# Sinkhorn chains regrouped: one GpSimd chain for six row tiles, joined in stages, and VectorE for the last four

## The chip, the core and the metric

The kernel runs on one core of one Trainium2 chip. A core has five engines with an instruction stream each: TensorE (PE, matmuls; PEld is its weight load), VectorE (DVE), ScalarE (ACT), GpSimd (POOL) and SyncE (SP, which issues the DMAs here). Every engine works off its own stream in order; an instruction that needs another engine's result waits for it, and everything behind it on its engine waits too.

The metric is the device time of one execution in microseconds (us), the median of several runs. The kernel before takes 1380.76 us (median of 3 runs, 1379.34 to 1381.67).

## The reference

The function is two transformer layers with adaptive layer norm, on x of two rows (batch entries) of 512 tokens by 512 channels. Layer 0 is a gated chunked linear attention and a sign-weight feed-forward; layer 1 is a softmax attention with 32 heads of width 16, and at its end a "hyper-connection" feed-forward with a Sinkhorn normalisation. Only that last part is touched here:

```python
def sinkhorn_log(logits, num_iters=50, tau=0.1):
    Z = logits / tau
    u0 = jnp.zeros(Z.shape[:-1], Z.dtype); v0 = jnp.zeros_like(u0)
    def step(carry, _):
        u, v = carry
        u = -jax.nn.logsumexp(Z + v[..., None, :], axis=-1)
        v = -jax.nn.logsumexp(Z + u[..., :, None], axis=-2)
        return ((u, v), None)
    (u, v), _ = jax.lax.scan(step, (u0, v0), None, length=num_iters)
    return jnp.exp(Z + u[..., :, None] + v[..., None, :])
...
x_norm = x * jax.lax.rsqrt(jnp.mean(x * x, axis=-1, keepdims=True) + RMS_EPS)
H_res  = sinkhorn_log((x_norm @ W_res.T).reshape(B, T, 4, 4) + H_res_base)
H_pre  = softmax(x_norm @ W_pre.T + H_pre_base);  H_post = softmax(x_norm @ W_post.T + H_post_base)
H_res  = (1 - g) * I + g * H_res                       # g = sigmoid(gate)
y      = einsum('btnc,btn->btc', x_streams, H_pre) @ W_branch
out    = einsum('btij,btjc->btic', H_res, x_streams) + einsum('btc,btn->btnc', y, H_post)
```

Every token has a 4 by 4 matrix, and 50 iterations turn it into a nearly doubly stochastic one. The result mixes the token's four streams of 128 channels.

## The kernel before

**Tiles and halves.** The 1024 tokens are eight tiles of 128 tokens (tokens on the partitions, 512 channels along the free axis), four for each batch row. The last part works on halves of a row, two tiles each. They are called A0 and A1 here (row 0, first and second half) and B0 and B1 (row 1).

**The order of the work.** Layer 1's attention runs over 16 steps in `order`, for row 0 and then row 1, in each for the first half of the queries and then the second. `piece()` issues one eighth of a step: score matmuls (L861) whose row maxima VectorE takes (L865), transposed score matmuls (L899) whose exponentials ScalarE takes (L904, shown as L78 with the tile `pt`), and the matmuls with the values (L919). After the last piece of a quarter, `weighed()` (L1357) puts the generator of that half's last part into the list `side` (L1379): `streams0` for A0 and A1, `streams1a` for B0, `streams1b` for B1. After every piece, `aside(2)` takes up to two steps (up to a `yield`) of each generator in the list, under `tc.high_priority(400)`. Instructions are so written in this order, and the framework's scheduler then lays out each engine's stream from its own model of times, by priority.

**One half's last part.** `opening` (L1001) makes the logits: transposes and matmuls on TensorE, statistics on VectorE, two small powers on GpSimd (L134, L135). With `last` the layer norm of the half is on VectorE (L1038, L1039), otherwise partly on GpSimd. `first_iteration` (L1115) does the first of the 50 iterations with logarithms and leaves a positive 4 by 4 matrix K per token. `branch` (L1053) is the branch with `W_branch`. `iterations` (L1141) does the other 49 in scaled form: fa = 1 / row sums of K fb, fb = 1 / column sums of K fa. `result` (L1178) makes the mixing matrix, and `mixed_on_tensor` (L1206) mixes one tile: for each of the 16 matrix entries ScalarE writes a diagonal 128 by 128 matrix (L1196) and TensorE multiplies it with a stream (L1217); with four more for the branch where that has not been added before (`branch_on_tensor`, L1198). `put` (L1188) multiplies with the gate on VectorE (L1191), adds the residual on GpSimd or VectorE (L1192) and stores the tile by a DMA on SP's queue.

**One iteration.** With `last` it is all on VectorE: multiply (L1164), sum (L1154), reciprocal (L1166), multiply (L1168), sum (L1154), reciprocal (L1170). Otherwise the multiplications are on GpSimd, and each sum is two additions there (L1157 for pairs, L1158 for the pairs' sums); only the two reciprocals are on VectorE. Such a GpSimd iteration is 6 GpSimd and 2 VectorE instructions and 4 hand-overs between the engines. Two tiles make operands of 32 elements per partition for K, 16 for the pairs, 8 for a factor. After the iterations in `renew` (16 and 32) K is made anew from the logits (`kernel_of`, L1146) with two Ln and an Exp on ScalarE.

**Who does which chain.** A0 and A1 are two separate GpSimd chains of 49 iterations on two tiles, each with a room of its own in memory (`chain_room`, L1093). B0 does iterations 1 to 16 alone on VectorE (`streams1a`). Then B0 and B1 share a room and 33 iterations on four tiles on VectorE (B0's 17 to 49 and B1's 1 to 33, L1289), and B1 does its last 16 alone (L1293). Behind B1's result one tile is mixed on TensorE and the other on VectorE (L1237) from a branch part that ScalarE has left in `foutb` (L1230).

Of the kernel before, what the change touches and what calls it, by code (L numbers as in the profile page):

```python
# [9 lines left out]
FP = mybir.dt.float32  # L10
# [6 lines left out]
UPS = 400, 400, 400, 400  # L17
RATES = None, None, None, None
HEAD = 16
UP = 400  # L20
RAW = 4
POP = 1
# [14 lines left out]
P = 128  # L37
B, L, HID = 2, 512, 512
NC = L // P
# [13 lines left out]
def tile_adaln(ctx: ExitStack, tc: tile.TileContext, a: dict, out: bass.AP):  # L53
# [117 lines left out]
    def temp(shape, dt, name, bufs=2):  # L171
        return wk.tile(shape, dt, name=name, bufs=bufs)
# [917 lines left out]
    over = lambda t: t.unsqueeze(3).to_broadcast(list(t.shape) + [NS])  # L1090
    along = lambda t: t.unsqueeze(2).to_broadcast([t.shape[0], t.shape[1], NS, NS])

    def chain_room(n, last):  # L1093

        room = temp([P, 512], FP, "sinkhorn", 4)
        used = [0]

        def carve(shape):
            m = int(np.prod(shape[1:]))
            t = room[:, used[0]:used[0] + m]  # L1100
            used[0] += m
            if len(shape) == 4:
                return t.rearrange("p (c i j) -> p c i j", i=NS, j=shape[3])
            return t.rearrange("p (c i) -> p c i", i=NS)

        R = {k: carve([P, n, NS, NS]) for k in ("z", "t", "y", "K")}
        R.update({k: carve([P, n, NS]) for k in ("mx", "s", "u", "v", "fa", "fb", "fl")})
        if not last:
            R["pairs"] = carve([P, n, NS, 2])
        return R  # L1110

    def part(R, lo, hi):
        return {k: t[:, lo:hi] for k, t in R.items()}

    def first_iteration(S, R):  # L1115
        z, t, y, K, mx, s_, u, v, fl = (R[k] for k in ("z", "t", "y", "K", "mx", "s", "u", "v", "fl"))
# [61 lines left out]
    def result(S, R):  # L1178

        hr, n = R["y"], S["n"]  # L1180
        nc.vector.tensor_tensor(hr, R["K"], over(R["fa"]), ALU.mult)
        nc.vector.tensor_tensor(hr, hr, along(R["fb"]), ALU.mult)
        hrf = hr.rearrange("p c i j -> p c (i j)")
        for c in range(n):
            nc.vector.scalar_tensor_tensor(hrf[:, c, :], hrf[:, c, :], gt[:, 0:1], diag, ALU.mult, ALU.add)
        S["hr"] = hr
# [55 lines left out]
        put(S, c, ff, ff, nc.gpsimd)  # L1242
        yield

    RENEW = 16, 32

    def streams0(c0):

        S = {"b": 0, "c0": c0, "n": 2}
        yield from opening(S, False)  # L1250
        R = chain_room(2, False)
        yield from first_iteration(S, R)
        yield from S["branch"]
        yield from iterations(R, range(1, NITER), RENEW, False)
        result(S, R)
        for c in range(2):
            yield from mixed_on_tensor(S, c, nc.gpsimd)

    joint = {}

    def streams1a():

        S = joint["a"] = {"b": 1, "c0": 0, "n": 2}
        yield from opening(S, True)
        R = joint["R"] = chain_room(4, True)
        yield from first_iteration(S, part(R, 0, 2))
        yield from S["branch"]
        yield from iterations(part(R, 0, 2), range(1, HEAD + 1), (HEAD,), True)

    def streams1b(ahead):  # L1270

        S = {"b": 1, "c0": 2, "n": 2}
        yield from opening(S, True)
        yield from ahead
        A, R = joint["a"], joint["R"]
        yield from first_iteration(S, part(R, 2, 4))

        def branches():
            yield from S["branch"]
            branch_on_tensor(S, 1)  # L1280
            yield
            branch_on_scalar(S, 0)
            yield
            for c in range(2):
                branch_on_tensor(A, c)
                yield

        side.append((1, branches(), UP))
        yield from iterations(R, range(1, NITER - HEAD), RENEW, True)  # L1289
        result(A, part(R, 0, 2))  # L1290
        side.append((None, mixed_on_tensor(A, 0, nc.gpsimd), UP))
        side.append((None, mixed_on_tensor(A, 1, nc.gpsimd), UP))
        yield from iterations(part(R, 2, 4), range(NITER - HEAD, NITER), RENEW, True)  # L1293
        result(S, part(R, 2, 4))
        last = [mixed_on_tensor(S, 1, nc.vector), mixed_on_vector(S, 0)]
        while last:
            for e in list(last):
                if next(e, "end") == "end":
                    last.remove(e)
            yield  # L1300
# [56 lines left out]
    def weighed():  # L1357
        w = wt[0]
        wt[0] += 1
        if w < n_pieces:  # L1360
            if w == n_pieces // 2:
                values1(1)
            weigh(order[w // 8], w % 8)
        o = w - OUT
        if 0 <= o < n_pieces and o % 4 == 3:
            outputs(o // 4)
        o -= 5
        if o >= 0 and o % 4 == 0 and o < n_pieces:
            j = o // 4
            finish(j)  # L1370
            if j % 16 == 5:
                with behind():
                    row_tiles(j // 16, (SB, CB, GB))
                    weights24(j // 16)
            if j % 8 == 7:
                k = j // 8
                if k == 2:
                    joint["ahead"] = streams1a()
                side.append((RATES[k], (streams0(2 * k) if k < 2 else joint["ahead"] if k == 2 else streams1b(joint["ahead"])), UPS[k]))  # L1379

    virtual = []
    load_stationary("wk0", 0, 0)
# [167 lines left out]
```

## Time and profile before

The profiled execution took 1379.86 us; its span, from the first to the last instruction, is 1378.0 us, so 1.9 us lie around it. All times below count from the span's start.

| event (profiled execution) | start, us |
|---|---|
| first GpSimd iteration of A0 (L1157) | 1093.16 |
| first GpSimd iteration of A1 (L1157) | 1172.59 |
| K of B0 there (L1136) | 1230.73 |
| iteration 33 of A0 (L1157) | 1243.90 |
| last matmuls with the attention's values (L919) | 1254.09 |
| K of B1 there (L1136) | 1267.94 |
| first joint sum of B0 and B1 (L1154, 128x64) | 1271.34 |
| A0's result (L1181) | 1291.19 |
| B0's result (L1181) | 1335.89 |
| A1's result (L1181) | 1339.96 |
| B1's result (L1181) | 1363.74 |
| last arithmetic instruction (L1192) | 1374.45 |
| end of the span | 1378.0 |

A timeline row reads: start, duration, engine, line, operation, out<-in, shapes of the output and the first input, count of merged instructions, and in brackets the idle time before it on its engine and what ended that. A row of the windows reads: the window, its length, and for each engine the busy microseconds and the number of instructions in it, then TensorE's granted clock and the DMA share.

### The profile page before, as it was taken

What the parts mean: (1) busy time and instruction counts of PE and PEld (TensorE: products, weight loads), DVE (VectorE), ACT (ScalarE), POOL (GpSimd) and SP (SyncE); (2) the same over time, 40 slices, a digit from 0 to 9 for tenths busy, and PEclk for the clock granted to TensorE, in tenths of its full rate; (3) what the DMA queues carried; (4) which work ended last, traced back from release to release, by engine and by line L of the source; (5) the groups of instructions that cost most, each with busy time, mean ns of one, the idle gap of its engine ahead of it and who ended that gap; (6) DMA issues with size and microseconds to landing.
All of it is one profiled execution on the core that took longest, in us unless ns stands there. A gap on an engine that the chain in (4) does not pass through costs nothing.

```text
span 1378.0 us, 22951 instructions
## 1 busy us (share of the span) xinstructions
PE 1249.1 (91%) x7224; PEld 1001.1 (73%) x7224; DVE 1109.9 (81%) x2732; ACT 847.2 (61%) x2384; POOL 783.8 (57%) x1218
## 2 busy tenths in 40 slices
PE   5989999999999999999989999699999999996308
PEld 2767888788788787888877887577777777764308
DVE  7999677787686778877989876577869889898887
ACT  5457576476366466766666665465758678775407
POOL 4465274365266367667788947634335755668651
PEclk9999999999999999999999999899999999997758
DMA  7122241231133143333443326613203321200001
GB/s 246 37 66 51 80 133 40 69 108 54 47 92 93 54 146 92 100 85 100 123 129 94 102 68 206 205 46 110 84 25 120 98 88 49 65 14 2 9 8 47
DMA packets 96369, 116.61 MB, mean 85 GB/s; under 512 B 12076, under 2 KB 51756, under 8 KB 96248
## 3 DMA queue, kind: packets, MB, share of 16 engines
q1 hardware_dynamic: 96248, 115.15, 27.8%
q8 instruction: 57, 0.93, 0.3%
q14 instruction: 64, 0.52, 0.1%
HBM read 101.59 MB, written 10.64 MB: 81 GB/s over the span
## 4 chain that ended last, share of the span: by engine, by line
PE 61%; DVE 16%; POOL 11%; DMA 4%; issue 4%; ACT 3%; SPq 1%; POOLq 0%; ACTq 0%; DVEq 0%
PE pps L251 12%; PE ops L251 10%; PE gps L251 9%; PE op L919 4%; PE s L899 4%; PE s L861 4%; PE yps L567 3%; PE mix L1217 3%; PE sps L251 2%; PE yps L569 2%; DVE m L865 2%; PE cps L251 2%; PE mps L290 1%; PE ztp L585 1%; POOL q L466 1%
## 5 line engine op out<-in xcount | busy, mean ns | idle before, releaser
L865 DVE TENSOR_REDUCE m<-s 128x1 f32<-128x512 f32 x256 | 165.4, 672 | 23.7 <-PE s L861 23.2
L78 ACT ACTIVATE pt<-s 128x512 f32<-128x512 f32 x256 | 138.0, 599 | 14.9 <-PE s L899 13.6
L466 POOL TENSOR_TENSOR q<-xcos,rot 128x512 f32<-128x512 f32 x64 | 92.5, 1445 | 60.4 <-DVE xcos L464 58.8
L78 ACT ACTIVATE sg<-sg 128x512 f32<-128x512 f32 x128 | 80.9, 633 | 61.2 <-DVE sg L497 59.3
L861 PE MATMUL s<-ks,qs 96*128 96x512 f32 x256 | 104.2, 438 | 10.0 <-DVE m L865 5.2
L251 PE MATMUL pps<-hh,wq_h 128*128 128x512 f32 x256 | 103.7, 405 | 3.4 <-ACT vT L785 3.2
L78 ACT ACTIVATE dec<-dec,room 128x128 f32<-128x128 f32 x256 | 82.9, 398 | 35.2 <-POOL dec L514 35.1
L251 PE MATMUL ops<-wo_h,zh 128*128 128x512 f32 x256 | 102.1, 399 | 0.7 <-DVE zl L590 0.7
L251 PE MATMUL ops<-wo_h,zl 128*128 128x512 f32 x256 | 101.7, 397 | 0.9 <-DVE zl L590 0.9
L251 PE MATMUL pps<-hl,wq_h 128*128 128x512 f32 x256 | 101.7, 397 | 0.0
L251 PE MATMUL gps<-wg_h,hh 128*128 128x512 f32 x256 | 101.6, 398 | 0.0
L251 PE MATMUL pps<-hh,wq_l 128*128 128x512 f32 x256 | 101.5, 397 | 0.0
L251 PE MATMUL gps<-wg_l,hh 128*128 128x512 f32 x256 | 101.0, 395 | 0.0
L567 PE MATMUL yps<-v,dec 128*128 128x128 f32 x512 | 94.3, 279 | 7.3 <-POOL wq_l L229 2.5
L899 PE MATMUL s<-qs,ks 100*128 100x256 f32 x512 | 98.9, 299 | 2.1 <-ACT pt L78 1.3
L251 PE MATMUL ops<-wo_l,zh 128*128 128x512 f32 x256 | 100.3, 392 | 0.0
L251 PE MATMUL gps<-wg_h,hl 128*128 128x512 f32 x256 | 100.3, 392 | 0.0
L514 POOL TENSOR_SCALAR_AFFINE_SELECT dec<-gb 128x512 f32<-128x512 f32 x64 | 49.2, 768 | 86.9 <-DMA gb<-g_dram 42.9
L534 POOL TENSOR_TENSOR gb<-gb,q 128x512 f32<-128x512 f32 x48 | 63.8, 1331 | 57.7 <-ACT gb L78 45.4
L899 PEld LDWEIGHTS s<-qs,ks 100*128 100x128 f32 x512 | 81.0, 192 | 19.8 <-ACT pt L78 5.9
L577 DVE SCALAR_TENSOR_TENSOR z<-yps,ss,sg 128x128 f32<-128x128 f32 x256 | 71.8, 341 | 27.2 <-ACT ss L78 26.9
L567 PEld LDWEIGHTS yps<-v,dec 128*128 128x128 f32 x512 | 79.5, 193 | 18.5 <-issue 4.9
(316 smaller groups left out, 3923.0 us busy)
## 6 DMA issues: line engine op xcount, KB each, us to landing
gb<-g_dram SPq DMA_DIRECT2D x64, 256.0 KB
raw<-in_wq SPq DMA_DIRECT2D x56, 256.0 KB
raw<-in_wg SPq DMA_DIRECT2D x48, 256.0 KB
raw<-in_wo SPq DMA_DIRECT2D x48, 256.0 KB
raw<-in_wmod SPq DMA_DIRECT2D x40, 256.0 KB
qs<-q_dram SPq DMA_DIRECT2D x64, 96.0 KB
q_dram<-hi SPq DMA_DIRECT2D x16, 256.0 KB
raw<-in_wk SPq DMA_DIRECT2D x14, 256.0 KB
```

The lines of the kernel that those rows point to most:

```text
L78: ins = nc.scalar.activation(o, i, func, **kw)
L251: nc.tensor.matmul(ps, lhsT=l, rhs=r, start=i == 0, stop=i == n - 1)
L466: nc.gpsimd.tensor_tensor(dst, sp(xc_), sp(rot), ALU.add)
L514: anchor["pool"] = nc.gpsimd.affine_select(out=dec, in_=gb, pattern=[[0, REP0], [1, P]], compare_op=ALU.is_ge, fill=-1e30, base=0, channel ...
L534: nc.gpsimd.tensor_tensor(gb, gb, q[:, c], ALU.mult)
L567: nc.tensor.matmul(yps[:, h, :], lhsT=u["pr"][:, h, :], rhs=u["v"][:, c, :], start=True, stop=not c)
L577: nc.vector.scalar_tensor_tensor(z[:, h, :], yps[:, h, :], ss[:, h:h + 1], sg[:, h * P:(h + 1) * P], ALU.mult, ALU.mult)
L861: anchor["pe"] = nc.tensor.matmul(ps, lhsT=st["qs"][rp][0:KS, i, qt * P:(qt + 1) * P], rhs=st["ks"][s][0:KS], start=True, stop=True,).ins
L865: anchor["dve"] = nc.vector.tensor_reduce(st["m"][:, 2 * qt + s, i:i + 1], ps, AX.X, ALU.max, negate=True).ins
L899: nc.tensor.matmul(ps[:, j, :], lhsT=st["ks"][s][0:KM, kt * P:(kt + 1) * P], rhs=st["qs"][rp][0:KM, i, :], start=True, stop=True,)
L919: mm = nc.tensor.matmul(op[32 * r:32 * r + 32, :], lhsT=va[st["b"]][kt // 2][:, kt % 2, 2 * st["t"] + r // 2, :], rhs=qd["pt"][r, kt // 2] ...
L1217: nc.tensor.matmul(mps[:, i], lhsT=dg[:, j], rhs=hv[:, j] if j < NS else yb[:, c], start=n > NS and j == 0, stop=j == n - 1 and (n > NS or ...
```

## The change

Rows are not regrouped, only who iterates when. A0, A1 and B0 share one GpSimd chain, `chain0`, that runs 65 iterations. A0 has its 1 to 49 in it, A1 comes in at 17 (its own 1) and stays to 65, B0 comes in at 33 and leaves after 48, which is its own sixteenth. The operands are so two tiles wide in iterations 1 to 16, four in 17 to 32, six in 33 to 48, four in 49 and two in 50 to 65. B0 then goes on with B1 on VectorE as before, and B1's generator does not issue the joint iterations until B0 has left the GpSimd chain. All eight tiles have one room, and K is renewed every 16 iterations of a chain; B1's last, lone stretch gets a renewal at its iteration 48 that it did not have. The results of A0 and A1 are mixed by generators of their own in `side`. A0, A1 and B0 have the new generator `front` for opening, first iteration and branch. `opening`, `first_iteration`, `iterations`, `result` and the mixing functions are as before.

```diff
 HEAD = 16
+STOP = 65, 65, 48
+POOLED = 65
...
-    def chain_room(n, last):
-
-        room = temp([P, 512], FP, "sinkhorn", 4)
+    def chain_room():
+
+        room = temp([P, 800], FP, "sinkhorn", 1)
...
+        n = B * NC
         R = {k: carve([P, n, NS, NS]) for k in ("z", "t", "y", "K")}
         R.update({k: carve([P, n, NS]) for k in ("mx", "s", "u", "v", "fa", "fb", "fl")})
-        if not last:
-            R["pairs"] = carve([P, n, NS, 2])
+        R["pairs"] = carve([P, n - 2, NS, 2])
         return R
 
     def part(R, lo, hi):
-        return {k: t[:, lo:hi] for k, t in R.items()}
+        return {k: t[:, lo:hi] for k, t in R.items() if hi <= t.shape[1]}
...
-    RENEW = 16, 32
-
-    def streams0(c0):
-
-        S = {"b": 0, "c0": c0, "n": 2}
-        yield from opening(S, False)
-        R = chain_room(2, False)
+    RENEW = tuple(range(HEAD, 2 * NITER, HEAD))
+    joint = {"S": [{"b": b, "c0": c0, "n": 2} for b in range(B) for c0 in (0, 2)]}
+
+    def front(k):
+
+        S = joint["S"][k]
+        R = part(joint["R"], 2 * k, 2 * k + 2)
+        yield from opening(S, k > 1)
         yield from first_iteration(S, R)
-        yield from S["branch"]
-        yield from iterations(R, range(1, NITER), RENEW, False)
-        result(S, R)
-        for c in range(2):
-            yield from mixed_on_tensor(S, c, nc.gpsimd)
-
-    joint = {}
-
-    def streams1a():
-
-        S = joint["a"] = {"b": 1, "c0": 0, "n": 2}
-        yield from opening(S, True)
-        R = joint["R"] = chain_room(4, True)
-        yield from first_iteration(S, part(R, 0, 2))
-        yield from S["branch"]
-        yield from iterations(part(R, 0, 2), range(1, HEAD + 1), (HEAD,), True)
-
-    def streams1b(ahead):
-
-        S = {"b": 1, "c0": 2, "n": 2}
-        yield from opening(S, True)
-        yield from ahead
-        A, R = joint["a"], joint["R"]
-        yield from first_iteration(S, part(R, 2, 4))
+        if k < 3:
+            yield from S["branch"]
+        S["there"] = True
+
+    def chain0():
+
+        R, H = joint["R"], joint["S"]
+        for it in range(1, POOLED + 1):
+            if it % HEAD == 1 and it // HEAD < 3:
+                while not H[it // HEAD].get("there"):
+                    yield
+            at_ = [k for k in range(3) if k * HEAD < it <= min(k * HEAD + NITER - 1, STOP[k])]
+            yield from iterations(part(R, 2 * at_[0], 2 * at_[-1] + 2), (it,), RENEW, False)
+            for k in at_:
+                if it == k * HEAD + NITER - 1:
+                    result(H[k], part(R, 2 * k, 2 * k + 2))
+                    for c in range(2):
+                        side.append((None, mixed_on_tensor(H[k], c, nc.gpsimd), UP))
+                elif it == STOP[k]:
+                    H[k]["over"] = True
+
+    def streams1b():
+
+        R, (A, S) = joint["R"], joint["S"][2:]
+        yield from front(3)
...
         side.append((1, branches(), UP))
-        yield from iterations(R, range(1, NITER - HEAD), RENEW, True)
-        result(A, part(R, 0, 2))
+        while not A.get("over"):
+            yield
+        yield from iterations(part(R, 4, 8), range(1, NITER - HEAD), RENEW, True)
+        result(A, part(R, 4, 6))
         side.append((None, mixed_on_tensor(A, 0, nc.gpsimd), UP))
         side.append((None, mixed_on_tensor(A, 1, nc.gpsimd), UP))
-        yield from iterations(part(R, 2, 4), range(NITER - HEAD, NITER), RENEW, True)
-        result(S, part(R, 2, 4))
+        yield from iterations(part(R, 6, 8), range(NITER - HEAD, NITER), RENEW, True)
+        result(S, part(R, 6, 8))
...
-                if k == 2:
-                    joint["ahead"] = streams1a()
-                side.append((RATES[k], (streams0(2 * k) if k < 2 else joint["ahead"] if k == 2 else streams1b(joint["ahead"])), UPS[k]))
+                if k == 0:
+                    joint["R"] = chain_room()
+                side.append((RATES[k], front(k) if k < 3 else streams1b(), UPS[k]))
+                if k == 0:
+                    side.append((RATES[k], chain0(), UPS[k]))
```

## The prediction

> **What bounds the kernel now.** I read the page's busy times and slices first, then windows cut where the chains change, then each engine's timeline in the tail.
>
> ```profile
> PE 1249.1 (91%) x7224; PEld 1001.1 (73%) x7224; DVE 1109.9 (81%) x2732; ACT 847.2 (61%) x2384; POOL 783.8 (57%) x1218
> ...
> PE   5989999999999999999989999699999999996308
> ...
> DVE  7999677787686778877989876577869889898887
> ```
>
> TensorE fills all but the last four slices. A chain matters there only where it delays what comes after the attention, and the last 128 us (from 1250) are the place of this change. The windows:
>
> ```profile
> 1172.00:1231.00 59.00, 58.37 (x535) 43.23 (x533) 52.60 (x171) 45.85 (x116) 38.09 (x174) 1.00 0.16 46
> 1231.00:1244.00 13.00, 12.65 (x128) 9.25 (x123) 12.12 (x63) 9.63 (x27) 7.79 (x37) 1.00 0.01 3
> 1244.00:1271.00 27.00, 14.50 (x125) 10.40 (x125) 23.66 (x155) 14.22 (x42) 23.00 (x103) 0.74 0.01 2
> 1271.00:1292.00 21.00, 3.83 (x17) 3.15 (x16) 18.51 (x102) 3.92 (x14) 18.36 (x96) 0.58 0.00 1
> 1292.00:1336.00 44.00, 12.87 (x80) 12.13 (x80) 36.97 (x176) 13.42 (x49) 24.34 (x98) 0.66 0.03 13
> ```
>
> After 1244 VectorE is 84 to 88% busy and TensorE nearly idle: a dependent chain of small VectorE operations sets the end. Its marks on VectorE's timeline are B0's K, the first joint sum, B1's result and the last arithmetic:
>
> ```profile
> 1230.73 0.19 DVE L1136 TENSOR_TENSOR sinkhorn<-sinkhorn 128x32 f32<-128x32 f32 x1
> ...
> 1271.34 0.21 DVE L1154 TENSOR_REDUCE sinkhorn<-sinkhorn 128x16 f32<-128x64 f32 x1
> ...
> 1364.54 0.38 DVE L1185 SCALAR_TENSOR_TENSOR sinkhorn<-sinkhorn,room 128x16 f32<-128x16 f32 x2
> ...
> 1373.72 0.69 DVE L1191 TENSOR_TENSOR fout<-mix,row 128x512 f32<-128x512 f32 x1 [1.79 <-PE mix L1217]
> ```
>
> So: B0 alone 40.6 us, joint 65.0 (to 1336.3), B1 alone 28.6 (to 1364.9), tail 13.1 (to 1378.0). The tail is ScalarE's: it makes A1's 40 diagonals from 1341.6, then 13 for the branch, then 48 for B0 and B1 to 1373.1, the last of which end the kernel.
>
> A GpSimd iteration's half, with hand-over, is best seen late, when little is in its way:
>
> ```profile
> 1313.19 0.24 POOL L1164 TENSOR_TENSOR sinkhorn<-sinkhorn 128x32 f32<-128x32 f32 x1 [0.31 <-DVE sinkhorn L1170]
> 1313.51 0.21 POOL L1157 TENSOR_TENSOR sinkhorn<-sinkhorn 128x16 f32<-128x16 f32 x1
> 1313.80 0.26 POOL L1158 TENSOR_TENSOR sinkhorn<-sinkhorn 128x8 f32<-128x8 f32 x1
> 1314.38 0.25 POOL L1168 TENSOR_TENSOR sinkhorn<-sinkhorn 128x32 f32<-128x32 f32 x1 [0.32 <-DVE sinkhorn L1154]
> ```
>
> Three dependent operations, the reciprocal on VectorE, and back. From 1310.93 to 1338.88 twelve iterations take 27.95 us: 2.33 each for two tiles, 1.17 a half. A lone VectorE iteration of two tiles takes 1.38 (1344.87 to 1346.25).
>
> **What the change removes.** GpSimd runs 65 iterations instead of 98, so 33 x 6 = 198 instructions of some 0.2 us go (part of them wider now), and VectorE loses 33 x 2 reciprocals for that, and B0's sixteen (16 x 6 instructions, of which 32 reciprocals stay merged into the chain's). Before 1250 I cost this at nothing: TensorE hides it, busy 58.37 of 59 us. Without that cover it would be at most 15 x 2 reciprocals by 0.2 us, 6 us of gain. After 1250 only what stands in the chain counts.
>
> **What it adds: B0's first sixteen iterations wait for, and run at the pace of, the GpSimd chain.** Step by step:
>
> 1. Iteration 17 needs A1's K, there for the GpSimd sum at 1172.6. Its sixteen iterations on four tiles are shown by no row. From below: one chain beside the attention took 41.76 us for eleven (1105.69 to 1147.45), 3.80 each. From above: A1's own sixteen beside A0's chain, 1172.59 to 1245.31, 4.55 each, with the GpSimd work of B0's opening in between. I take 4.2, as the merged chain has half the instructions of the second row but waits behind the same maxima (L865, 0.6 us a piece, in VectorE's in-order stream): 67.2 us, to 1239.8. Renewal at 32: A0's took 3.5 us (Ln at 1240.43, next sum 1243.90), 2.5 more than a plain reciprocal. So iteration 33 starts at 1242.3, where A0's did before at 1243.9. B0's K, there at 1230.7, waits 11.6 us. Bounds 1235.9 and 1247.9.
> 2. Iterations 33 to 48 on six tiles, also not shown. GpSimd takes about 1.28 us for 512 elements and 0.245 for 32: 2.16 ns an element. A half gets 64 + 32 + 16 more elements: 0.24 us. VectorE's reciprocal takes 0.20 for 8 elements and 0.245 for 16, so 24 cost 0.1 more. A half is 1.17 + 0.34, an iteration 3.0; sixteen are 48.2, less 0.5 for the first, which has no multiplication. B1's opening gets in the way: from 1257.26 to 1265.91 the GpSimd chains made two iterations in 8.65 us instead of 2 x 2.63 (1268.55 to 1279.08 for four), so 3.4 more. End 1293.4. Bounds for an iteration: 2.33 (width free) and 3.95 (as three chains side by side, from 2.63 for two): 10.7 less, 15 more. I stay at 3.0, as the 0.24 comes from the same operation on the same engine.
> 3. Renewal at 48 with an Exp on ScalarE, about 2.0 us: first joint sum at 1295.4 instead of 1271.3, **24.1 us later**. Behind it on VectorE stand all joint iterations, and TensorE, ScalarE and SP have nothing else that could end the kernel.
>
> The rule that speaks against the move: a lone GpSimd iteration is 2.33 us against VectorE's 1.38, a factor 1.69 by these rows. The Trainium skill (GPSIMD Engine Reference, Engine selection) puts two-input elementwise work at about twice VectorE's time; by it B0's sixteen would be an estimated 2 x 16 x 1.38 = 44 us on two tiles, where the rows give 37. The rule that speaks for the merging: VectorE: DVE Perf Modes (The TRN2 errata) says that operations on SBUF pay a fixed cost per instruction, which few large ones spread better; it names VectorE and ScalarE, and GpSimd's 0.245 us for 32 elements beside 0.20 for 8 looks the same here. Were all of it fixed, step 2 would be 37 us; by the rows it is 48.
>
> **Joint stretch, 65.0 before.** Beside one GpSimd chain a joint iteration takes 1.733 (thirteen in 22.53 us from 1309.68), beside two some 1.80, beside none about 1.62. A1's 17 remaining iterations last some 44 us beside it. So eleven iterations win 0.07 each and the last eight 0.11: -1.6. A1's two outputs, which fell into B1's lone stretch, now fall here: each 0.6 us of L1191 and 0.83 more for the L1168 beside GpSimd's L1192 (1.03 instead of 0.21, at 1351.79 and 1357.25): +2.9. Together +1.3.
>
> **Lone stretch, 28.6 before.** A1's outputs leave (2.9, and 1.5 for which VectorE waited on their matmuls at 1350.73). B0's two come in, since its 32 diagonals by 0.295 are done 9.4 us after its result: +2.9. The new renewal at 48 costs 1.0 net, as the second joint one did (2.13 from L1168 to the next sum, 1.1 without). Together -0.5.
>
> **Tail, 13.1 before.** ScalarE no longer has A1's diagonals ahead of it: 16 x 0.295 = 4.7 for B1's tile, 0.6 for TensorE, and from its end to the span's end 4.3 as before, with some 0.7 for starts and for the other tile's L1191: 10.3. **-2.8.** The outputs' DMAs are the same eight on SP's queue, the early ones in other places; in the last 38 us the queue moved 1.6 MB, so no transfer queues behind another long.
>
> **Sum.** 24.1 + 1.3 - 0.5 - 2.8 = 22.1 us. The profiled execution took 1379.86 us (span 1378.0 and 1.9 around), 0.9 below the median: 1402 us.
>
> **Rivals.**
>
> *The head is not late (not slower).* With its reciprocals let through promptly the merged chain reaches 33 when B0's K comes, 1230.7; that takes 3.48 us an iteration in 17 to 32, below the 3.80 row. With width free as well, 2.33 an iteration: 1230.7 + 36.8 + 3.4 + 2.0 = 1272.9, 1.6 late; all together -0.4: 1379.5, and below that if B1's opening disturbs less. It decides where the chain leaves iteration 48 before some 1271. For it: VectorE has fewer reciprocals then. Against: VectorE, 52.6 of 59 us busy in 17 to 32, keeps its maxima, and both lower bounds must hold.
>
> *Width is nearly free, only step 2:* 1402 - 10 = 1392. *Width costs like separate chains:* 1402 + 15 = 1417. The 512-element rows lie between.
>
> *The chains do not run beside each other.* All eight tiles share a room; if the framework orders GpSimd's part against VectorE's, A1's 17 last iterations (2.33 each) stand between the joint ones: +40, 1442. Against: B0 and B1 shared a room, and B1's first iteration (L1122 at 1264.79) ran between B0's operations with no wait.
>
> **How the numbers follow.** Forecast 65%, head not late 7%, width nearly free 15%, width dear 10%, chains in lock step 3%. The range 1387 to 1414 holds the forecast with one bound of either step at a time and most of the cheap-width case; it leaves out the first rival, lock step and part of the dear case. Time tells a change of 0.2%, 2.8 us, from none. The first rival is split 4% faster, 3% same: slower 93%.
>
> **What would show it.** In the new profile: the first 128x64 sum (L1154) near 1295; iteration 33, the first GpSimd pair sum of 48 elements, near 1242; from there 3 us an iteration; VectorE half idle between 1244 and 1295; no long wait of the last L1191 on diagonals. I am wrong if the 128x64 sum starts before 1280, or if the joint iterations take other than 1.6 to 1.75 us.

## The result

| kernel | time, us, median (runs) | range, us |
|---|---|---|
| before (run beside the changed one) | 1380.74 (4) | 1379.34 to 1381.67 |
| after | 1402.25 (4) | 1401.24 to 1403.04 |

The ratio is 1.0156, 95% interval 1.0139 to 1.0174: the change costs 21.5 us. The profiled execution has a span of 1400.2 us instead of 1378.0. Lines of the changed kernel up to its L1239 stand two lower than in the kernel before (the joint sum is L1156, GpSimd's pair sum L1159, the last `put` L1193).

The profile after, first the busy times and slices of the page:

```profile
PE 1246.4 (89%) x7224; PEld 1001.5 (72%) x7224; DVE 1102.5 (79%) x2570; ACT 848.1 (61%) x2384; POOL 757.9 (54%) x1021
...
PE   5979999999999999999989997799999999981443
...
DVE  7999678687687687787988966668788888853887
```

GpSimd has 197 instructions fewer, VectorE 162 fewer, and yet the span is longer. The two slices where VectorE drops to 5 and 3 (the 36th and 37th, 1225 to 1295 us) are new. Then the windows, which have for each engine PE, PEld, DVE, ACT, POOL the busy time and the number of instructions:

```profile
1172.00:1239.00 67.00, 66.32 (x626) 49.04 (x624) 59.05 (x171) 51.98 (x133) 33.97 (x121) 1.00 0.14 40
1244.00:1271.00 27.00, 13.85 (x116) 10.04 (x115) 11.78 (x51) 12.41 (x35) 15.92 (x50) 0.69 0.01 2
1271.00:1296.00 25.00, 1.47 (x9) 1.08 (x8) 6.25 (x22) 2.82 (x11) 14.07 (x51) 0.57 0.00 0
1296.00:1340.00 44.00, 15.88 (x96) 15.23 (x96) 38.48 (x186) 15.82 (x54) 25.14 (x102) 0.66 0.03 13
```

Between 1271 and 1296 no engine is busy for more than 14.07 of 25 us. A chain in which two engines take turns fills neither. Its marks, on GpSimd's timeline iteration 33, where B0 is taken in:

```profile
1242.88 0.27 POOL L1159 TENSOR_TENSOR sinkhorn<-sinkhorn 128x48 f32<-128x48 f32 x1 [1.03 <-ACT sinkhorn L80]
```

and on VectorE's B0's K, the first joint sum, B1's result and the last `put`:

```profile
1226.84 0.20 DVE L1138 TENSOR_TENSOR sinkhorn<-sinkhorn 128x32 f32<-128x32 f32 x1
...
1295.88 0.22 DVE L1156 TENSOR_REDUCE sinkhorn<-sinkhorn 128x16 f32<-128x64 f32 x1 [0.41 <-ACT sinkhorn L80]
...
1387.99 0.38 DVE L1187 SCALAR_TENSOR_TENSOR sinkhorn<-sinkhorn,room 128x16 f32<-128x16 f32 x2
...
1395.89 0.69 DVE L1193 TENSOR_TENSOR fout<-mix,row 128x512 f32<-128x512 f32 x1 [2.59 <-PE mix L1219]
```

B0's K is there at 1226.84 and waits 16.0 us for iteration 33. The joint sum is 24.5 us later than before (1295.88 for 1271.34). From there on little changes: the joint stretch, to the first multiplication on B1 alone (1361.71), takes 65.8 us instead of 65.5, the lone one (to 1388.37) 26.7 instead of 28.1, the tail 11.8 instead of 13.1. The sum 24.5 + 0.3 - 1.4 - 1.3 is the 22 us of the span. What is to be explained lies between B0's K and the joint sum.

On GpSimd's timeline one iteration of six tiles in the quiet part:

```profile
1271.79 0.35 POOL L1166 TENSOR_TENSOR sinkhorn<-sinkhorn 128x96 f32<-128x96 f32 x1 [0.42 <-DVE sinkhorn L1172]
1272.22 0.27 POOL L1159 TENSOR_TENSOR sinkhorn<-sinkhorn 128x48 f32<-128x48 f32 x1
1272.57 0.22 POOL L1160 TENSOR_TENSOR sinkhorn<-sinkhorn 128x24 f32<-128x24 f32 x1
1273.21 0.39 POOL L1170 TENSOR_TENSOR sinkhorn<-sinkhorn 128x96 f32<-128x96 f32 x1 [0.42 <-DVE sinkhorn L1168]
...
1274.66 0.35 POOL L1166 TENSOR_TENSOR sinkhorn<-sinkhorn 128x96 f32<-128x96 f32 x1 [0.42 <-DVE sinkhorn L1172]
```

From 1271.79 to 1274.66: 2.87 us. The bracket says that GpSimd stands idle 0.42 us in every half for VectorE's reciprocal. And one iteration beside B1's opening, which takes 7.08 us (1256.02 to 1263.10):

```profile
1256.02 0.86 POOL L1166 TENSOR_TENSOR sinkhorn<-sinkhorn 128x96 f32<-128x96 f32 x1 [0.41 <-DVE sinkhorn L1172]
...
1260.81 0.40 POOL L1170 TENSOR_TENSOR sinkhorn<-sinkhorn 128x96 f32<-128x96 f32 x1 [2.14 <-DVE lg L1037]
...
1263.10 0.35 POOL L1166 TENSOR_TENSOR sinkhorn<-sinkhorn 128x96 f32<-128x96 f32 x1 [0.53 <-DVE sinkhorn L1119]
```

The multiplication L1170 waits while VectorE works on B1's opening. The reciprocal that it needs stands behind the layer norm and the logits in VectorE's stream, as its timeline shows:

```profile
1258.96 1.41 DVE L1041 SCALAR_TENSOR_TENSOR h<-h,rstd,row 128x512 f32<-128x512 f32 x2
1260.28 0.24 DVE L1037 SCALAR_TENSOR_TENSOR lg<-lg,rstd,room 128x24 f32<-128x24 f32 x1
1260.43 0.30 DVE L1168 RECIPROCAL sinkhorn<-sinkhorn 128x24 f32<-128x24 f32 x1
```

GpSimd's own statistics for that opening (L136, L137) stand between the sums as well.

### The profile page after: what moved, and what is told of

Read it like the earlier page. It is cut to its first block, busy times and chain, and to the rows that moved or that the text cites. A ratio compares the mean times of both kernels' runs of the same rounds, so it can differ in the third digit from the quotient of the medians.

```text
span 1400.2 us, 22613 instructions
## 1 busy us (share of the span) xinstructions
PE 1246.4 (89%) x7224; PEld 1001.5 (72%) x7224; DVE 1102.5 (79%) x2570; ACT 848.1 (61%) x2384; POOL 757.9 (54%) x1021
## 5 line engine op out<-in xcount | busy, mean ns | idle before, releaser
L80 ACT ACTIVATE pt<-s 128x512 f32<-128x512 f32 x256 | 138.2, 598 | 14.8 <-PE s L901 13.1
L1219 PE MATMUL mix<-h,dg 128*128 128x128 f32 x224 | 40.2, 342 | 75.5 <-ACT dg L1198 75.4
```

The costliest lines, as they stand in the source:

```text
L80: ins = nc.scalar.activation(o, i, func, **kw)
L1219: nc.tensor.matmul(mps[:, i], lhsT=dg[:, j], rhs=hv[:, j] if j < NS else yb[:, c], start=n > NS and j == 0, stop=j == n - 1 and (n > NS or ...
```

## The experiments

My theory: the loss is B0's head on GpSimd, by two parts, the wait for row 0's iteration 32 and the pace of six tiles. Rivals: the merging itself, new renewals, GpSimd's own load, or the tail. The main part of the program shifts by some us from one profile to the next (A0's K comes at 1089.9 to 1096.8, ahead of everything the edits touch), so this table counts the joint sum from A0's K. Each time has its own ratio to the kernel before, run on the same chip; that one's median lay between 1380.49 and 1381.41 us, so a difference between times of two rows carries up to 0.9 us of that. Runs 3, 4 and 6 to 9 leave iterations of A0 and A1 out and are no versions to use; they price parts of the changed kernel.

| kernel | time, us | ratio to before (95%) | A0's K | joint sum | joint sum from A0's K |
|---|---|---|---|---|---|
| before | 1380.74 | | 1092.04 | 1271.34 | 179.3 |
| after | 1402.25 | 1.0156 (1.0139 to 1.0174) | 1091.34 | 1295.88 | 204.5 |
| 1 merging only | 1382.07 | 1.0014 (1.0004 to 1.0024) | 1093.71 | 1271.59 | 177.9 |
| 2 merging, no late renewal | 1378.78 | 0.9988 (0.9974 to 1.0002) | 1093.35 | 1271.24 | 177.9 |
| 3 no wait | 1389.52 | 1.0067 (1.0053 to 1.0081) | 1093.17 | 1284.55 | 191.4 |
| 4 two wide, 33 to 48 | 1385.80 | 1.0038 (1.0025 to 1.0052) | 1095.44 | 1286.14 | 190.7 |
| 5 three chains | 1398.68 | 1.0130 (1.0109 to 1.0152) | 1089.91 | 1287.76 | 197.9 |
| 6 no wait, 33 to 48 two wide | 1389.21 | 1.0064 (1.0041 to 1.0087) | 1094.49 | 1286.21 | 191.7 |
| 7 wait kept, 34 to 47 two wide | 1392.11 | 1.0082 (1.0063 to 1.0101) | 1091.06 | 1285.58 | 194.5 |
| 8 two wide, 33 to 47, 48 on six | 1383.33 | 1.0011 (0.9994 to 1.0028) | 1093.71 | 1277.55 | 183.8 |
| 9 the same, 26 to 31 left out | 1380.49 | 0.9998 (0.9988 to 1.0009) | 1093.36 | 1275.32 | 182.0 |

**1. Merging only: B0's head back on VectorE.** A0 and A1 stay one chain.

```diff
@@ front(k)
+        if k == 2:
+            yield from iterations(R, range(1, HEAD + 1), (HEAD,), True)
+            S["over"] = True
@@ chain0
-            if it % HEAD == 1 and it // HEAD < 3:
+            if it % HEAD == 1 and it // HEAD < 2:
...
-            at_ = [k for k in range(3) if ...]
+            at_ = [k for k in range(2) if ...]
```

> The change with one part undone: B0's first sixteen iterations are on VectorE again, while A0 and A1 keep their merged GpSimd chain. My theory, that the loss is B0's head waiting for and running at the pace of the GpSimd chain: the first joint sum comes near 1268 (1264 to 1272), as VectorE has fewer reciprocals of A0 and A1 to serve than before, A1's matrices are ready near 1330 instead of 1342, the tail is some 1.3 us shorter, and the time is 1376 us (1372 to 1380). The rival that merging itself (one room, A1 bound to A0's pace, more renewals) costs part of the loss: 1385 us or more, and the joint sum still near 1271.

1382.07 us: 20.2 of the 21.5 us are gone, so the head's move is the loss and the merging isn't. My size was missed all the same. The joint sum came only 1.4 us earlier than before (177.9 for 179.3), A1's result was there at 1339.6 where I had expected 1330, and all four puts of A1 and B0 fell into the lone stretch. VectorE's timeline shows A1's first put, B1's renewal, B0's two puts and B1's result:

```profile
1350.45 0.69 DVE L1193 TENSOR_TENSOR fout<-mix,row 128x512 f32<-128x512 f32 x1 [1.99 <-PE mix L1219]
...
1364.84 0.19 DVE L1149 TENSOR_TENSOR sinkhorn<-sinkhorn 128x32 f32<-128x32 f32 x1
1365.09 0.69 DVE L1193 TENSOR_TENSOR fout<-mix,row 128x512 f32<-128x512 f32 x1
...
1366.11 1.14 DVE L1150 TENSOR_TENSOR sinkhorn<-sinkhorn 128x32 f32<-128x32 f32 x1
1367.17 0.68 DVE L1193 TENSOR_TENSOR fout<-mix,row 128x512 f32<-128x512 f32 x1
...
1369.96 0.38 DVE L1187 SCALAR_TENSOR_TENSOR sinkhorn<-sinkhorn,room 128x16 f32<-128x16 f32 x2
```

Between the renewal and the result, which were 2.5 us apart in the changed kernel (1385.50 to 1387.99), lie 5.1 us. Two puts are in them, and two small operations that take 1.14 us (L1150) and 1.02 us (L1170, at 1368.21) where the changed kernel's took 0.19 and 0.21; each runs beside the 512-element addition of a put on GpSimd (L1194, at 1365.91 and 1367.93).

**2. The same without the renewal after B1's iteration 48** (the lone stretch renews after 16 and 32 only, as before the change).

```diff
-        yield from iterations(part(R, 6, 8), range(NITER - HEAD, NITER), RENEW, True)
+        yield from iterations(part(R, 6, 8), range(NITER - HEAD, NITER), (16, 32), True)
```

> As the merge alone, and B1's lone stretch has no renewal at its iteration 48, as in the kernel before. My theory: about 1.2 us less than the merge alone (renewal 1.4 us by the changed kernel's trace, less the multiplication of 0.2), so 1375 us, the lone stretch shorter by as much. The rival that the renewal is hidden behind ScalarE's diagonals of B0: no difference.

1378.78 us, an interval that takes in no change. The renewal and what falls behind it cost 3.3 us, measured as the difference of the two medians, where I had priced it at 1.0 net.

**3. No wait: the chain leaves out iterations 26 to 31** of A0 and A1.

```diff
         for it in range(1, POOLED + 1):
+            if 26 <= it <= 31:
+                continue
```

> The changed kernel without iterations 26 to 31 of the GpSimd chain (left out for A0 and A1, so their result has six iterations less), so that the chain is at iteration 33 before B0's K is there. B0 then does not wait the 12 to 16 us for the chain. My theory: iteration 33 starts near 1229 and runs beside the attention's maxima at some 4.3 us an iteration until 1240, then at 2.87; first joint sum near 1287 instead of 1296, time 1393 us (1389 to 1396). The rival that only the six-tile pace counts and the start does not: 1400 to 1402. The rival that all of the wait comes back: 1387.

Iteration 33 is now B0's to decide, on GpSimd's timeline:

```profile
1229.51 0.27 POOL L1159 TENSOR_TENSOR sinkhorn<-sinkhorn 128x48 f32<-128x48 f32 x1 [2.18 <-DVE sinkhorn L1140]
```

The bracket names B0's first iteration (L1140) where it was row 0's renewal. The joint sum is 13.1 us nearer to A0's K, the time 12.7 us less: the wait costs that much.

**4. Two wide: iterations 33 to 48 on B0's tiles alone** (A0 and A1 leave those out).

```diff
-            yield from iterations(part(R, 2 * at_[0], 2 * at_[-1] + 2), (it,), RENEW, False)
+            wide = [2] if 33 <= it <= 48 else at_
+            yield from iterations(part(R, 2 * wide[0], 2 * wide[-1] + 2), (it,), RENEW, False)
```

> The changed kernel with iterations 33 to 48 of the GpSimd chain on B0's two tiles alone (left out for A0 and A1). The instructions are as many, but a third as wide. My theory: an iteration takes 2.33 us instead of 2.87 between 1268 and 1294, the first joint sum comes some 8.6 us earlier, near 1287, and the time is 1393.5 us (1391 to 1396). The rival that the fixed cost of instructions and hand-overs is all of it: 1401 to 1402. The rival that six tiles cost like three chains: 1385 or less.

1385.80 us where I expected 1393.5. Two things were in this edit that I had not seen. B0's first sum on its own tiles ran at 1231.35, 14.8 us before row 0's renewal at 32 (1246.19): an instruction on B0's tiles alone depends on nothing of row 0, so the wait was gone with the width. And A0 and A1, with nothing between their 32 and 49, went on beside B0 (A0's result at 1250.49, for 1296.85 in the changed kernel). So this run isn't the width's price; runs 7 to 9 separate these.

**5. Three chains, nothing merged:** A0's and A1's as before the change, and B0's sixteen as a third GpSimd chain.

```diff
@@ front(k), in place of chain0
+        if k < 2:
+            yield from iterations(R, range(1, NITER), (16, 32), False)
+            result(S, R)
+            for c in range(2):
+                yield from mixed_on_tensor(S, c, nc.gpsimd)
+        elif k == 2:
+            yield from iterations(R, range(1, HEAD + 1), (HEAD,), False)
+            S["over"] = True
```

> Three chains of sums on GpSimd and nothing merged: A0's and A1's chains as before the change, and B0's first sixteen iterations as a third chain that starts at its own exponential and waits for nobody. My theory, that GpSimd is one engine with about 4 us of its own work for three halves' iterations wherever they are put, expects the three to interleave at about 3.95 us for one iteration of each, so that the first joint sum comes at about 1298 us, as late as with the merged chain (1295.88), and the time is 1403 us (1396 to 1410). The rival, that waiting for the merged chain's iteration 33 and the six-tile width are what costs, expects the joint sum back near 1276 us and about 1383 us.

Neither sum nor time met either expectation: the joint sum came at 1287.76, 6.6 us nearer to A0's K than with the merged chain and 18.6 further than before the change. The window before it:

```profile
1265.00:1287.00 22.00, 4.32 (x20) 3.94 (x20) 9.27 (x52) 5.52 (x20) 21.92 (x124) 0.58 0.00 1
```

GpSimd is busy 21.92 of 22 us: here the engine itself is the bound, as I held, but it isn't shared evenly. B0's sixteen took 58.3 us from its K (1227.27) to its renewal (1285.60), 3.65 each, and A0's and A1's results came 5.0 us later than before (1296.15 and 1344.99), 7.1 us counted from A0's K. The time is down only 3.6 us, as the lone stretch has four puts in it (1354.94 to 1373.65), where the changed kernel has two, and takes 30.0 us for 26.7. This run computes everything and has neither the wait nor the width, and it still takes 17.9 us more than before (1398.68 for 1380.74): a head on GpSimd beside two other chains is dear by itself. So the wait and the width, which the other runs price, are what the merged chain pays; without the merging the loss takes another form.

**6. No wait, and 33 to 48 two wide.** The edits of 3 and 4 together.

> Both cuts at once: the chain leaves out its iterations 26 to 31, so that B0 is joined earlier, and A0 and A1 leave out their iterations 33 to 48, so that B0's sixteen are done on its two tiles alone. If the loss is the wait for iteration 33 plus the width, as I hold, the two gains add up: first joint sum about 1277 us (1274 to 1280) and time about 1379 us (1376 to 1384). If a part of the loss lies elsewhere (in the renewals at both joints, in the tail), the time stays at 1388 us or above though both are taken away.

1389.21 us, outside my range and above what edit 4 gave alone. A0's result was there at 1227.22, before B0's K. Its 80 mixing matmuls ran between 1231 and 1254, among those of B1's attention, whose last matmul came at 1262.6, for 1253.1 in run 8. And A1, which nothing held back either, had its last iterations on GpSimd beside B0's (A1's result at 1282.73, for 1320.99 in run 8). One window, in this run and then in run 8, where row 0 was held back:

```profile
1250.00:1265.00 15.00, 12.92 (x136) 9.33 (x128) 5.82 (x28) 11.15 (x27) 12.64 (x59) 1.00 0.10 37
```

```profile
1250.00:1265.00 15.00, 5.76 (x52) 3.72 (x50) 8.29 (x36) 5.16 (x14) 10.42 (x36) 0.73 0.00 1
```

136 matmuls for 52, and 59 GpSimd instructions for 36. B1's K came 181.0 us behind A0's K here, 172.1 in run 8. But the joint sum came 10.7 us behind that K (1286.21 for 1275.52), so it waited for B0's head, which took 55.3 us from B0's K to the joint sum, 48.3 in run 8. How much of that is A0's mixes and how much A1's iterations isn't separated.

**7. The width alone: 33 and 48 on six tiles, 34 to 47 on B0's two.** Iteration 33 keeps the wait, 48 keeps A0 and A1 from running ahead.

```diff
-            yield from iterations(part(R, 2 * at_[0], 2 * at_[-1] + 2), (it,), RENEW, False)
+            wide = [2] if 34 <= it <= 47 else at_
+            yield from iterations(part(R, 2 * wide[0], 2 * wide[-1] + 2), (it,), RENEW, False)
```

> The width alone, with the wait kept: chain iterations 33 and 48 on all six tiles, so that B0 waits for row 0's iteration 32 and row 0 for B0's last, and 34 to 47 on B0's two tiles (A0 and A1 leave those out). If 33 starts near 1242.9 us as in the changed kernel and an iteration of six tiles costs 2.87 us where two cost 2.33, this saves 14 x 0.54 = 7.6 us: first joint sum near 1288.3 us, time 1394.5 us (1392 to 1398). If the opening of row 1's second half and not the width holds the chain, the sum stays at 1293 or later; if the wait was already gone in the two-wide runs and was nearly all of their gain, likewise.

GpSimd's timeline, two halves on two tiles and the first on six:

```profile
1279.29 0.24 POOL L1166 TENSOR_TENSOR sinkhorn<-sinkhorn 128x32 f32<-128x32 f32 x1 [0.32 <-DVE sinkhorn L1172]
...
1280.42 0.25 POOL L1170 TENSOR_TENSOR sinkhorn<-sinkhorn 128x32 f32<-128x32 f32 x1 [0.32 <-DVE sinkhorn L1168]
...
1281.55 0.35 POOL L1166 TENSOR_TENSOR sinkhorn<-sinkhorn 128x96 f32<-128x96 f32 x1 [0.32 <-DVE sinkhorn L1172]
```

2.26 us on two tiles where six took 2.87. Iterations 34 to 47 take 36.0 us (1245.52 to 1281.55) instead of 46.0 (1245.81 to 1291.86): 14 x 0.61 = 8.5 by the steady pace, and 1.5 less lost beside the attention's end and B1's opening. The time is 10.1 us less. The width costs that.

**8. Two wide from 33, and 48 on six.** The wait is gone as in 4, but A0 and A1 are held until 48.

```diff
-            yield from iterations(part(R, 2 * at_[0], 2 * at_[-1] + 2), (it,), RENEW, False)
+            wide = [2] if 33 <= it <= 47 else at_
+            yield from iterations(part(R, 2 * wide[0], 2 * wide[-1] + 2), (it,), RENEW, False)
```

> Chain iterations 33 to 47 on B0's two tiles alone, and iteration 48 again on all six, so that A0 and A1 can't run ahead on GpSimd as they did with 33 to 48 two wide; A0 and A1 leave out iterations 33 to 47. My theory, that each iteration of six tiles takes 2.87 us where two take 2.33 (two hand-overs of 1.17 us), expects 15 x 0.54 = 8.1 us: first joint sum near 1287.8 us instead of 1295.9, time 1394 us (1391 to 1398). The rival, that the width cost nothing and the earlier gain came from A0 and A1 being done early, expects a joint sum at 1294 or later and 1401 us or more.

I expected the wait to stay; it went. GpSimd's timeline has B0's sums (128x16) between row 0's (128x32) from the start:

```profile
1229.51 0.22 POOL L1159 TENSOR_TENSOR sinkhorn<-sinkhorn 128x16 f32<-128x16 f32 x1 [0.34 <-DVE m L1063]
...
1233.08 0.27 POOL L1159 TENSOR_TENSOR sinkhorn<-sinkhorn 128x32 f32<-128x32 f32 x1
...
1233.92 0.22 POOL L1159 TENSOR_TENSOR sinkhorn<-sinkhorn 128x16 f32<-128x16 f32 x1
```

So this is the run for both costs at once: 18.9 us less time and a joint sum 20.7 nearer to A0's K, of 12.7 + 10.1 = 22.8 that the two cost one by one. The difference of 3.9 in time is not taken apart further; with the wait gone, more of B0's iterations run beside the attention and row 0's chain.

**9. The same without iterations 26 to 31** of A0 and A1.

> The same, and the chain leaves out its iterations 26 to 31 as well, so that B0 doesn't wait. If the wait (11.3 us, measured alone) and the width (8.1 us by working) add up and nothing else holds the joint back, the joint sum comes near 1276.5 us and the time is 1383 us (1379 to 1387). If something else holds it once both are gone (the attention of B1, or GpSimd itself), the joint sum stays at 1282 us or later and the time at 1387 us or above, as when both were cut without the lock.

1380.49 us, 0.9998 of before. With wait and width taken away in the merged chain, nothing of the loss is left in the time (with 21 iterations of A0 and A1 left out for it). Of the 25.2 us by which the joint sum had moved away from A0's K, 22.5 are back; the time is back in full, as the changed kernel's lone stretch and tail are shorter.

**10. Can the lone stretch of experiment 2 be cleared of puts?** The mixes of A0, A1 and B0 get priority 0 instead of 400, which moves them in the written order.

```diff
-                        side.append((None, mixed_on_tensor(H[k], c, nc.gpsimd), UP))
+                        side.append((None, mixed_on_tensor(H[k], c, nc.gpsimd), 0))
```

> The version with the head back on VectorE and without the late renewal (1378.78 us), with the mixes of row 0's two halves and of row 1's first taken into the order ahead of other filling work, so that their puts on VectorE leave the lone stretch of row 1's second half. If the puts in the lone stretch are what keeps that stretch at its length, it gives 1375 us (1372 to 1379). If the puts' place is set by the end of the mixes anyway, the time stays at 1378.8 us.

1379.54 us, ratio 0.9993 (0.9976 to 1.0011): no change. B0's first put stands at 1368.01, 27.8 us behind its result (1340.25); without the edit it was 26.4 (1337.47 to 1363.90).

**11 and 12. B0 back on GpSimd once A0 is done.** The rows suggest the opposite of the change: head on VectorE, where B0 is alone and late work waits for it, and B0's last iterations on GpSimd, where A0's place is free. B0 and B1 are joined for ten (11) or thirteen (12) iterations, B0 then goes beside A1 on GpSimd, and B1 has VectorE.

```diff
@@ streams1b
-        yield from iterations(part(R, 4, 8), range(1, NITER - HEAD), RENEW, True)
...
+        yield from iterations(part(R, 4, 8), range(1, GIVE + 1), (GIVE,), True)
+        A["given"] = True
+        yield from iterations(part(R, 6, 8), range(GIVE + 1, NITER), (GIVE, 30), True)
@@ chain0, behind iteration 48 of A0 and A1
+        yield from iterations(part(R, 0, 2), (NITER - 1,), RENEW, False)
+        done(0)
+        while not H[2].get("given"):
+            yield
+        n = HEAD + 1
+        yield from iterations(part(R, 2, 6), range(NITER - 1, NITER - 1 + n), (NITER - 2,), False)
+        done(1)
+        yield from iterations(part(R, 4, 6), range(HEAD + GIVE + n + 1, NITER), (), False)
+        done(2)
```

> A version of my own that computes everything: B0's head stays on VectorE, B0 and B1 are joined there for ten iterations only, and B0 then goes over to GpSimd, where it takes A0's place beside A1 when A0 is done (17 iterations four tiles wide, then B0's last six alone), while B1 has VectorE for its last 39. From the rows: the joint stretch has 10 x 1.98 us instead of 33 x 1.98, the lone one 39 x 1.72 instead of 16 x 1.72, so B1's result comes 23 x 0.26 = 6 us sooner, and B0's on GpSimd by about 1296 + 17 x 2.6 + 6 x 2.33 = 1354 us, before B1's. Time 1374 us (1371 to 1379). If the lone chain on VectorE is slowed by the reciprocals of GpSimd's chain and by the puts as much as by two more tiles, it stays at 1379 us or above.

> The version that hands B0 back to GpSimd after ten joint iterations, with thirteen instead: B1 should lose 3 x 0.26 = 0.8 us, and B0, which has three fewer iterations alone on GpSimd, should be ready about 6 us sooner, near 1354 us, ahead of B1. If B0's late result was what kept the tail at 16.7 us, the time comes to 1375 us (1372 to 1378). If it is TensorE's mixes of three halves in a row from 1344 us on that end last, it stays at 1379 us.

1379.55 us (ratio 0.9985, 0.9976 to 0.9994) and 1379.53 us (0.9983, 0.9971 to 0.9995). These two beat both kernels, but the kernel before only by an estimated 2.1 and 2.4 us, by the ratios, which is below 0.2%. In the second, B0's result is ready at 1352.5, 6.6 us sooner than in the first (1359.1), about as I expected, and B1's at 1357.1, 7.8 us sooner than before the change and 3.6 sooner than in the first (1360.7), where the results of both halves met on VectorE. The spans are the same all the same, 1377.4 and 1377.5. The second one's window behind B1's result, and its last `put` on VectorE's timeline:

```profile
1358.00:1366.00 8.00, 8.00 (x57) 8.00 (x56) 7.87 (x19) 8.00 (x28) 2.64 (x3) 1.00 0.17 66
```

```profile
1373.15 0.69 DVE L1193 TENSOR_TENSOR fout<-mix,row 128x512 f32<-128x512 f32 x1 [3.98 <-PE mix L1219]
```

TensorE, its weight load and ScalarE are busy all of the 8 us: the mixes of A1, B0 and B1 now stand in a row from 1346.0, and the last `put` waits 3.98 us for them. ScalarE sets their pace: 28 diagonals in 8.00 us are 0.286 each, and two matmuls go with each. What the chain won is given back there, as the rival of run 12 said.

## Why the prediction was right

The forecast was 1402 us and the time 1402.25; the bound, its place and its cause hold. That the sum of 22.1 us met the span's 22.2 so closely is luck in part: its four terms were off by +0.4, -1.0, -0.9 and +1.5 us, which cancel. By its steps:

**Before 1250: right on the end, short on the way.** I costed the 198 GpSimd instructions that go at nothing, and the time of experiment 1 agrees. But B0's K did come forward: 135.5 us behind A0's K instead of 138.7. VectorE's lighter load is the likely reason, though three unmerged chains, which have no such relief, also show 137.4. That gain went into the wait, and in experiment 1 only 1.4 us of it reached the joint sum.

**Step 1, iteration 33 at 1242.3: 1242.88.** Iterations 17 to 32 took 4.28 us each, from 1170.83 to 1239.2, for the 4.2 I took between 3.80 and 4.55. K's wait was 16.0 instead of 11.6 us, mostly because K came earlier (by 3.9 us), and only by 0.6 because iteration 33 came later. Experiment 3 shows that this wait is a cost of its own: 12.7 us.

**Step 2, 3.0 us an iteration plus 3.4: right sum of two misses.** The pace was 2.87, and 5.8 us were lost between 1248.7 and 1263.1, which the starts of the iterations show: three of them took 3.73, 3.60 and 7.08, 14.4 us for 3 x 2.87 = 8.6. The step's misses, about -2 and +2.4, cancel. Of the 5.8 us, 4.2 are beside B1's opening, for the 3.4 that I took. The other 1.6 fall in the two iterations ahead of it, beside the attention's last normalisations on VectorE (L947, L949) and additions on GpSimd (L955), which had no term in my sum. The opening's part was mis-sized. That a single merged chain suffers more from a late reciprocal, as it has no other GpSimd work to do meanwhile, is my reading of the 4.2; no run tries it. Experiment 7 shows the pace's part of the loss (10.1 us with two tiles), so the rival that width is nearly free falls, and the price per element was near, if high: I took 0.14 us for 64 more elements, and 128x96 took 0.35 to 0.39 us, 0.10 to 0.14 more than 128x32.

**Step 3, joint sum at 1295.4: 1295.88.** Its renewal took 1.5 us from the last reciprocal (1294.35), for 2.0.

**Joint and lone stretch.** +1.3 was +0.3, and -0.5 was -1.4. A1's two puts fell into the joint stretch (1354.19 and 1356.48) and B0's two into the lone one (1371.31 and 1373.37), as I had it; why both came out shorter than I said isn't taken apart. The undisturbed joint iteration is 1.66 us (1315.72 to 1319.03 for two), inside the band I gave.

**Tail: -2.8 was -1.3.** This is the term that was mis-sized in its mechanism too. I let ScalarE's 16 diagonals end it, 0.6 us for TensorE behind them. The diagonals went as fast as I said, 4.88 us from 1388.46 to 1393.34; but the chain of waits of the changed kernel ends on TensorE:

```profile
1388.46 1.87 ACT dg L1198 x6
1390.38 5.48 PE mix L1219 x30
1395.89 0.70 DVE fout L1193
```

The last matmul is done at 1395.86, 2.5 us behind ScalarE. The windows of the changed kernel's tail, whole and then from the 30 matmuls on, cut where the granted clock changes:

```profile
1388.00:1396.00 8.00, 6.26 (x32) 5.78 (x32) 5.38 (x20) 4.88 (x16) 1.27 (x1) 0.61 0.06 25
1390.38:1394.30 3.92, 3.92 (x18) 3.92 (x19) 2.88 (x10) 2.96 (x10) 0.92 (x1) 0.50 0.00 0
1394.30:1395.85 1.55, 1.55 (x14) 1.35 (x12) 0.00 (x0) 0.00 (x0) 0.34 (x1) 1.00 0.23 90
```

and of the tail before:

```profile
1364.80:1374.00 9.20, 8.89 (x61) 8.70 (x60) 7.41 (x21) 8.35 (x29) 3.89 (x3) 1.00 0.08 31
```

At a granted clock of 0.50, 18 matmuls took 3.92 us, 0.22 each, and two are more than a diagonal of 0.305. At 1.00, from 1394.30 on, 14 took 1.55 us, 0.11 each. ScalarE had finished 0.96 us before that change, so the faster pace isn't its doing. In the tail before, at 1.00, 61 matmuls went with 29 diagonals of 0.288 us, two to each: there ScalarE set the pace, as I had read it. So the mis-sized part is the 0.6 us that I gave TensorE behind the diagonals, 2.5 as measured, and the rows put it on the clock. Ahead of this tail TensorE had stood idle for 16.47 us (1372.45 to 1388.92); ahead of the tail before, its windows show it busy for 22.07 of 25 us (1339.80 to 1364.80). That the idle time is why the clock was low agrees with these rows and was not tried by itself.

**The rivals.** "Head not late" needed iteration 33 at 1230.7; it came 12.2 us later. "Width dear" (3.95 an iteration) falls by 2.87, though three chains side by side do come near it (3.65, run 5). Lock step fell: the joint iterations ran at 1.66 beside A1's last.

**My own expectations of the runs** missed where I read the order of the code as a wait. In 4 and 8 I took a written order for a dependence. In 6 I left out that a chain which isn't held back sends its mixes and its last iterations to engines that someone else's path needs. In 1 I had A1 ready 9.6 us too early, and with it A1's puts out of the lone stretch.

## What to carry to other kernels

Merging chains into one wider instruction stream also merges their dependences: a tile that joins waits for the slowest member's point in the chain, and that wait (12.7 us here) is as dear as the wider operations (10.1 us), even while each engine is busy half the time. Not merging is no way out where the engine is then full: three chains side by side still lost 17.9 us. Move work to a slower engine where it has slack behind it, not at the head of the chain that sets the end. When a bound is pulled in, price what it uncovers first: here 7.8 us of a faster chain came to 0.5 us in the span because the mixes on TensorE and ScalarE became the last to end.

## What the hardware showed that I had not expected

- Width on GpSimd costs less than its count, and hand-over costs much: 96 elements per partition took 0.35 to 0.39 us for 0.24 at 32, and its idle time per half for VectorE's reciprocal, 0.42 us on six tiles and 0.32 on two, is as long as an operation.
- TensorE's small matmuls (128x128 by 128x128, f32) took 0.22 us each at a granted clock of 0.50 and 0.11 at 1.00, within one tail. With one 0.29 us diagonal of ScalarE for every two of them, ScalarE is the slower engine at 1.00 and TensorE at 0.50.
- With A0 and A1 merged, B0's K comes 135.5 to 136.4 us behind A0's in every profile, for 138.7 before and 137.4 with three chains, though TensorE is busy 66.32 of 67 us there. With some 30 reciprocals fewer on VectorE ahead of it, the K is 1 to 3 us earlier; that they are the reason is not tried by itself.
- The 1.0 us that a small VectorE multiplication takes instead of 0.2 beside GpSimd's 512-element addition hits the path itself in run 11, twice in a row: 1.15 us at 1356.76 and 1.04 at 1359.26 (L1184), each beside an L1194 of 1.3 us on GpSimd.
